# Turned probabilities in two single banks, and a scheduler with other costs, in an encoder-decoder layer

## The chip, the cores and the metric

The kernel runs on one core of a Trainium2 chip. The metric is the device time of one execution in microseconds (us). The time of the kernel before is the median of three runs.

## The reference

The reference is one encoder layer over a short context (2 x 77 x 512) and one decoder layer over a long input `x` (2 x 2048 x 512), all in float32, with 16 heads of 32 and a feed-forward width of 2048. What it computes, cut to its core:

```python
eb = _rel_bias(enc_rel, Ts, Ts)
x = src                                    # the context, 77 rows
x = x + _mha(ln1(x), ln1(x), enc_in, enc_out, eb)
x = x + relu(ln2(x) @ enc_ff1.T + b) @ enc_ff2.T + b
memory = x
sb = _rel_bias(dec_rel_self, Tt, Tt) + causal
cb = _rel_bias(dec_rel_cross, Tt, Ts)
y = tgt                                    # the input, 2048 rows
y = y + _mha(ln1(y), ln1(y), dec_sa_in, dec_sa_out, sb)
y = y + _mha(ln2(y), memory, dec_ca_in, dec_ca_out, cb)
y = y + relu(ln3(y) @ dec_ff1.T + b) @ dec_ff2.T + b
return y

# _mha: q, k, v projections; scores = q @ k.T / sqrt(32) + bias;
# softmax over the keys; times v; output projection
```

The relative bias has one value for all keys at a distance of 128 rows or more, so only the last two key tiles of a query tile need a bias of their own.

## The kernel before, in words

**Stages.** The causal self-attention comes first, with the encoder, the projections and the layer norms placed among its work. The cross attention and the feed-forward follow; there the products are done in seven instead of eight block products, with TensorE as one full array. In the profile the first stage ends at about 1560 us.

**Units.** The self-attention is cut into 128 units: two batches, four blocks of 512 rows (`m`), four groups of four heads (`g`) and four tiles of 128 query rows (`t`). A unit of block `m` and tile `t` has 4m + t + 1 key tiles, so the largest have 16, which is 2048 keys; the last unit, number 127, is one of these. Each unit goes through four kinds of work:

- *score* (`scores`, line 1002): for up to four key tiles, one matmul for each of the four heads, each on 32 rows of the array and into a bank of PSUM of its own, so four banks at a time. DVE then moves each bank into the area `pp` and keeps the running maximum (its tiles `pp` and `mx`); after the last piece it forms the negative maximum `nm`.
- *exp*: one ACTIVATE for each head on ACT, over all keys of the unit, in place in `pp`.
- *turn* (`turn`, line 1057): for up to two key tiles, the probabilities of four heads are transposed on TensorE, 64 query rows at a time, 16 transposes in all. The lower and the upper 64 rows go to two banks. Each bank is copied into its half of a tile `pts`, by ACT or by DVE (`copy` offers both).
- *value* (`values`, line 1081): for the same key tiles, matmuls with 32 output rows for each head, all of a group into one bank that stays held over the group's four units.

TensorE so works in four tilings: 64x128 for transposes, 32x128 for scores, 128x32 for values and projections, and 128x128. In the profile a matmul in float32 counts as two instructions, a transpose as one.

**Banks.** PSUM has eight banks of 512 columns. `Places` (its `grab` is line 128) hands them out when a task starts. A slot of two places takes an even-odd pair where one is free and comes free as a whole; a slot of one takes a place whose neighbour is taken, where there is one. A place comes free when the last task that uses the slot has ended.

**Who sets the order.** Nothing in the kernel's text fixes the order of the work. A `Tape` records every operation as part of a task, with the tasks that it depends on. A task has a kind, a unit and a part of the unit, and these give its key through the table `PLAN`. Then `plan` (line 402) runs the tasks through a clock of its own, on the host, before anything is built: SyncE, ACT, DVE and GpSimd take the ready task of the lowest key in `pick` (line 514); TensorE has one candidate for each tiling in `choices` (line 532), and for each of them, and for two short pauses, `ahead` (line 562) plays the next 20 us and adds up the work that TensorE, DVE and ACT would get done. The best is taken. The result is one fixed order of instructions for each engine, which `run` emits; all of them therefore carry line 360 in the profile. The chip never consults the planner: its costs act only through the order, and through the choice between ACT and DVE for some evictions.

What the planner believes of the chip stands in a few constants: `cost_of` (line 227) for durations; `SWITCH` (line 60), added to a task of TensorE whose tiling differs from that of the one before; `LATER` (line 61), the time from a task's end until another engine can use its result; and in `start` (line 585) one queue for transfers, each with 1300 ns to begin, its bytes at 190 a nanosecond, and 700 ns to land. `PLAN` holds nine sets of parameters, one for each 16 units and one for what follows.

Of the kernel before, what the change touches and what calls it, by code (L numbers as in the profile page):

```python
# [43 lines left out]
for _n, _w in _VECS:  # L44
# [15 lines left out]
SWITCH = {(32, 128): 217, (128, 32): 139, (64, 128): 140, (128, 128): 217}  # L60
LATER = {"PE": 212, "DVE": 130, "ACT": 150, "POOL": 110, "SP": 60}
# [4 lines left out]
LOOK = {"look":20000.0,"pause":(150.0,400.0)}  # L66
PLAN = [
    {"window": 6.9, "hold": 2.5, "flex": 271,
     "stay": {(64, 128): 0.463, (128, 32): 0.15, (32, 128): 0.337, (128, 128): 0.322},
     "keys": {"score": (-2.08, 0.76), "exp": (-0.5, 0.2), "turn": (0, 0.93), "value": (1.75, 1.12), "light": (-0.98, 0.02), "job": (0.33, 0.33), "late": (-0.6, 0), "stats": (-0.5, 0), "load": (0.04, 0.13), "ff": (0.42, 0), "side": (-0.28, 0)}},  # L70
    {"window": 5.9, "hold": 1.59, "flex": 305,
     "stay": {(64, 128): 0.588, (128, 32): 0.35, (32, 128): 0.195, (128, 128): 0.33},
     "keys": {"score": (-2.65, 0.76), "exp": (-0.19, 0.2), "turn": (0, 1.0), "value": (0.7, 1.56), "light": (-0.37, 0.02), "job": (0.45, 0.31), "late": (-0.6, 0), "stats": (-0.5, 0), "load": (0.04, 0.38), "ff": (-0.32, 0), "side": (-0.47, 0)}},
    {"window": 3.5, "hold": 0.97, "flex": 234,
     "stay": {(64, 128): 0.588, (128, 32): 0.462, (32, 128): 0.782, (128, 128): 0.322},
     "keys": {"score": (-2.44, 0.76), "exp": (0.02, 0.2), "turn": (0, 0.86), "value": (0.7, 0.96), "light": (-0.1, 0.02), "job": (0.16, 0.31), "late": (-0.6, 0), "stats": (-0.5, 0), "load": (0.03, 0.38), "ff": (-0.32, 0), "side": (-0.28, 0)}},
    {"window": 6.6, "hold": 0.89, "flex": 54,
     "stay": {(64, 128): 0.362, (128, 32): 0.368, (32, 128): 0.375, (128, 128): 0.259},
     "keys": {"score": (-2.91, 0.87), "exp": (-0.28, 0), "turn": (0, 0.86), "value": (1.16, 1.46), "light": (-0.37, 0.02), "job": (0.29, 0.31), "late": (-0.6, 0), "stats": (-0.5, 0), "load": (0.06, 0.38), "ff": (-0.32, 0), "side": (-0.28, 0)}},
    {"window": 6.5, "hold": 2.17, "flex": 34,  # L80
     "stay": {(64, 128): 0.36, (128, 32): 0.35, (32, 128): 0.195, (128, 128): 0.33},
     "keys": {"score": (-2.08, 0.76), "exp": (-0.19, 0.2), "turn": (0, 0.86), "value": (0.83, 1.56), "light": (-0.37, 0.02), "job": (0.45, 0.31), "late": (-0.6, 0), "stats": (-0.5, 0), "load": (0.04, 0.38), "ff": (-0.32, 0), "side": (-0.87, 0)}},
    {"window": 5.9, "hold": 2.46, "flex": 117,
     "stay": {(64, 128): 0.36, (128, 32): 0.35, (32, 128): 0.195, (128, 128): 0.633},
     "keys": {"score": (-2.65, 0.76), "exp": (-0.19, 0.2), "turn": (0, 0.89), "value": (0.7, 1.56), "light": (-0.37, 0.02), "job": (0.45, 0.31), "late": (-0.6, 0), "stats": (-0.5, 0), "load": (0.04, 0.38), "ff": (0.17, 0), "side": (-0.47, 0)}},
    {"window": 5.2, "hold": 0.97, "flex": 259,
     "stay": {(64, 128): 0.396, (128, 32): 0.462, (32, 128): 0.782, (128, 128): 0.322},
     "keys": {"score": (-2.44, 0.76), "exp": (0.02, 0.2), "turn": (0, 0.86), "value": (0.7, 0.96), "light": (-0.1, 0.02), "job": (0.16, 0.31), "late": (-0.6, 0), "stats": (-0.5, 0), "load": (0.03, 0.38), "ff": (-0.32, 0), "side": (-0.28, 0)}},
    {"window": 3.5, "hold": 0.89, "flex": 54,
     "stay": {(64, 128): 0.362, (128, 32): 0.368, (32, 128): 0.375, (128, 128): 0.259},  # L90
     "keys": {"score": (-2.91, 0.87), "exp": (-0.28, 0), "turn": (0, 0.86), "value": (1.16, 1.46), "light": (-0.37, 0.02), "job": (0.29, 0.31), "late": (-0.6, 0), "stats": (-0.5, 0), "load": (0.06, 0.38), "ff": (-0.32, 0), "side": (-0.28, 0)}},
    {"window": 5.9, "hold": 1.95, "flex": 305,
     "stay": {(64, 128): 0.214, (128, 32): 0.35, (32, 128): 0.195, (128, 128): 0.33},
     "keys": {"score": (-2.65, 0.76), "exp": (-0.19, 0.2), "turn": (0, 0.97), "value": (0.7, 1.56), "light": (-0.37, 0.02), "job": (0.45, 0.31), "late": (-0.6, 0), "stats": (-0.5, 0), "load": (0.04, 0.38), "ff": (-0.32, 0), "side": (-0.47, 0)}},
]
# [27 lines left out]
class Places:  # L123
# [103 lines left out]
def cost_of(engine, op, a, k):  # L227
    out = a[0]
    F = max(free_of(x) for x in a[:2] if is_ap(x))
    if engine == "PE":  # L230
# [5 lines left out]
        stream, load = n * 2 / 2.4, 63 if passes == 1 else 117 * cols / P  # L236
# [54 lines left out]
class Tape:  # L291
# [70 lines left out]
    def prepare(self):  # L362
# [10 lines left out]
        for t in tasks:  # L373
# [11 lines left out]
            t.by = dict(t.ways)  # L385
# [6 lines left out]
            if t.ways[0][0] == "SP":  # L392
                a = t.ways[0][1][0][2][0]
                t.size = free_of(a) * a.shape[0] * 4
# [7 lines left out]
    def plan(self, parts, look=0.0, weights=(1.0, 0.5, 0.5), pause=()):  # L402
# [3 lines left out]
        for t in tasks:  # L406
            t.todo, t.came, t.at = len(t.before), 0.0, None
            kind, n, part = t.kind
            t.part = parts[min(max(int(n), 0) // (NC * TB), len(parts) - 1)]
            first, wide = t.part["keys"][kind]  # L410
            t.key = n + first + wide * part
# [5 lines left out]
        self.left = sorted(tasks, key=lambda t: (t.key, t.order))  # L417
        run = Run(self)
        for t in tasks:
            if not t.todo:  # L420
                run.ready(t)
        gain = dict(zip(("PE", "DVE", "ACT"), weights))
        while len(run.order) < len(tasks):
            run.step_events()
            while True:
# [6 lines left out]
                if look:  # L432
                    best = None
                    for t in found + list(pause if len(found) > 1 or found[0].mode != run.mode else ()):
                        mark = run.save()
                        score = run.ahead(t, look, gain)
# [3 lines left out]
                    run.take(best[1])  # L440
# [6 lines left out]
class Run:  # L447
# [3 lines left out]
    def __init__(self, tape):  # L451
        self.tape, self.left, self.floor, self.now = tape, tape.left, 0, 0.0
# [3 lines left out]
        self.mode, self.dma, self.share, self.period, self.worked = None, 0.0, 0.5, 0, {}  # L456
        self.events, self.frees, self.order, self.log = [0.0], [], [], None
        self.places = list({id(s.places): s.places for s in tape.slots}.values())

    def save(self):  # L460
        self.log = []
        return (
            self.floor, self.now, dict(self.free), dict(self.port), {e: list(v) for e, v in self.lists.items()}, self.mode, self.dma,
# [4 lines left out]
    def back(self, mark):  # L468
# [3 lines left out]
        (self.floor, self.now, self.free, self.port, self.lists, self.mode, self.dma, self.share, self.period, self.worked,  # L472
# [41 lines left out]
    def pick(self, e):  # L514
# [3 lines left out]
        limit, now = low.key + low.part["window"], self.now  # L518
        shut = e in self.port and self.port["DVE" if e == "POOL" else "POOL"] > now
        for key, _, t in self.lists[e]:  # L520
            if key > limit:
                return None
            if t.came > now or shut and e in t.port or any(u.seen > now and u.by != e for u in t.banks):
# [3 lines left out]
            if e == "DVE" and len(t.ways) > 1 and self.free["ACT"] < now + low.part["flex"]:  # L527
# [4 lines left out]
    def choices(self):  # L532
# [3 lines left out]
        rule, now = low.part, self.now  # L536
        limit, stay, hold = low.key + rule["window"], rule["stay"], rule["hold"]
        wait, found = {}, {}
        for key, _, t in self.lists["PE"]:
            if key > limit:  # L540
                break
            if t.came > now or any(u.seen > now and u.by != "PE" for u in t.banks):
# [12 lines left out]
    def take(self, first):  # L555
        if isinstance(first, float):
# [28 lines left out]
    def start(self, e, t):  # L585
# [3 lines left out]
        took = t.spans[e]  # L589
        if e == "PE":  # L590
# [5 lines left out]
            at, stop, p = now, now + took, int(now // PERIOD)  # L596
            while at < stop:
                to = max(at, min(stop, (p + 1) * PERIOD))
                self.worked[p] = self.worked.get(p, 0.0) + (to - at) * t.dense
                at, p = to, p + 1  # L600
            if t.mode != self.mode:
                self.mode = t.mode
                took += SWITCH[t.mode]
        end = t.until = now + took
# [6 lines left out]
        seen = end + LATER[e]  # L611
        if e == "SP":
            self.dma = max(self.dma, now + 1300) + t.size / 190.0
            seen = self.dma + 700
        for u in t.banks:
            put(u, "by", e)
            put(u, "seen", seen)
        for s in t.fresh:
            put(s, "at", s.places.grab(s.n))
        for s in t.slots:  # L620
            put(s, "left", s.left - 1)
            if not s.left:
                heapq.heappush(self.frees, (seen, id(s), s))
        events = self.events
        heapq.heappush(events, seen)
        heapq.heappush(events, end)
        for w in t.after:
            came = end if e in w.own else seen
# [7 lines left out]


# [43 lines left out]
def tile_encoder_decoder(ctx: ExitStack, tc: tile.TileContext, ins, out):  # L681
# [102 lines left out]
    with (  # L784
# [272 lines left out]
        def turn(n, k0, kn):  # L1057

            pts = turned_places.take(kn)
            rows = P // 2  # L1060
            pair = bank(2)
# [1225 lines left out]
```

## Time and profile before

| what | value |
|---|---|
| median of three runs | 2637.32 us (2636.71 to 2638.04) |
| the profiled execution's own time | 2637.01 us |
| its span, first to last instruction | 2635.2 us |
| mean granted clock of TensorE | 0.997 |
| TensorE busy | 2607.7 us, 99% of the span |
| DVE, ACT, GpSimd busy | 1789.6, 1506.8, 774.5 us |

The profile is of one execution. Its page gives each engine's busy time, the chain of work that ended last, and groups of instructions with their mean duration and the idle time before them. Matmuls are pipelined and their ends are modelled: the end of a run of matmuls lies some way after the start of the next run, so that a change of tiling shows as busy time, and only a longer wait as idle time. The pitch of matmuls is therefore read from start to start. A row of the timeline merges instructions of one group that follow each other.

### The profile page before, as it was taken

What the parts mean: (1) busy time and instruction counts of PE and PEld (TensorE: products, weight loads), DVE (VectorE), ACT (ScalarE), POOL (GpSimd) and SP (SyncE); (2) the same over time, 40 slices, a digit from 0 to 9 for tenths busy, and PEclk for the clock granted to TensorE, in tenths of its full rate; (3) what the DMA queues carried; (4) which work ended last, traced back from release to release, by engine and by line L of the source; (5) the groups of instructions that cost most, each with busy time, mean ns of one, the idle gap of its engine ahead of it and who ended that gap; (6) DMA issues with size and microseconds to landing.
All of it is one profiled execution on the core that took longest, in us unless ns stands there. A gap on an engine that the chain in (4) does not pass through costs nothing.

```text
span 2635.2 us, 83740 instructions
## 1 busy us (share of the span) xinstructions
PE 2607.7 (99%) x35326; PEld 1777.3 (67%) x35326; DVE 1789.6 (68%) x5181; ACT 1506.8 (57%) x2890; POOL 774.5 (29%) x697
## 2 busy tenths in 40 slices
PE   9999999999999999999999999999999999999999
PEld 4456555555555455555555667888888888888898
DVE  4776588888887687788788874647373737373634
ACT  2665478778877567678778764343434343434331
POOL 1110151100001011202000013828374746465546
PEclk9999999999999999999999999999999999999999
DMA  8333363310115222423010244545556554545466
GB/s 220 94 92 110 113 187 99 103 54 19 42 46 138 81 70 62 152 80 118 23 46 18 77 141 133 179 154 167 166 160 186 162 175 151 180 145 172 141 204 200
DMA packets 252714, 320.28 MB, mean 122 GB/s; under 512 B 29569, under 2 KB 142513, under 8 KB 252211
## 3 DMA queue, kind: packets, MB, share of 16 engines
q1 hardware_dynamic: 252338, 314.93, 39.2%
q8 instruction: 278, 4.55, 0.7%
q14 instruction: 98, 0.79, 0.1%
HBM read 274.91 MB, written 39.95 MB: 119 GB/s over the span
## 4 chain that ended last, share of the span: by engine, by line
PE 93%; DVE 4%; ACT 2%; issue 1%; POOL 0%; DMA 0%; POOLq 0%; DVEq 0%; ACTq 0%
PE psum L360 93%; DVE pp L360 3%; ACT pp L360 1%; DVE pts L360 1%; ACT nT L360 0%; POOL pp L360 0%; ACT pts L360 0%; DVE oT L360 0%; DMA xt<-in_x_dram 0%; DVE bnst L360 0%; POOL vv L360 0%; ACT kT L360 0%; DVE nm L360 0%; DVE xr L360 0%; DVE kT L360 0%
## 5 line engine op out<-in xcount | busy, mean ns | idle before, releaser
L360 ACT ACTIVATE pp<-pp,nm 128x128 f32<-128x128 f32 (+15 forms) x512 | 615.0, 1209 | 115.6 <-DVE nm L360 114.2
L360 DVE TENSOR_SCALAR_CACHE_REDUCE pp<-psum 128x512 f32<-128x512 f32 (+3 forms) x1024 | 561.6, 591 | 129.6 <-PE psum L360 128.1
L360 ACT COPY pts<-psum 128x512 f32<-128x512 f32 (+2 forms) x785 | 405.4, 571 | 277.1 <-PE psum L360 229.4
L360 PEld LDWEIGHTS psum<-ident,pp 64*128 64x128 f32 (+1 forms) x8904 | 320.6, 139 | 189.6 <-issue 67.0
L360 PE MATMUL psum<-ident,pp 64*128 64x64 f32 (+1 forms) x8904 | 381.2, 228 | 8.8 <-DVE pp L360 4.1
L360 POOL TENSOR_TENSOR pp<-pp 128x512 f32<-128x512 f32 (+1 forms) x196 | 264.3, 1358 | 359.4 <-DMA pp<-in_dec_ff_wT_dram 169.7
L360 DVE COPY pts<-psum 128x512 f32<-128x512 f32 (+2 forms) x479 | 298.8, 657 | 80.5 <-PE psum L360 75.5
L360 PE MATMUL psum<-pp 128*128 128x128 f32 (+4 forms) x2984 | 352.5, 282 | 0.2 <-DVE oT L360 0.2
L360 PEld LDWEIGHTS psum<-pp 128*128 128x128 f32 (+3 forms) x2984 | 334.0, 190 | 23.7 <-issue 13.9
L360 PE MATMUL psum<-kT,q 32*128 32x512 f32 (+3 forms) x2560 | 334.3, 575 | 3.1 <-DVE pp L360 1.7
L360 PE MATMUL psum<-pts,vv 128*32 128x128 f32 x8704 | 319.6, 277 | 3.8 <-ACT pts L360 1.7
L360 PEld LDWEIGHTS psum<-pts,vv 128*32 128x32 f32 x8704 | 220.0, 109 | 113.7 <-issue 80.6
L360 PE MATMUL psum<-vv,pp 128*128 128x256 f32 (+1 forms) x1072 | 256.4, 390 | 0.0
L360 PE MATMUL psum<-nT,wqk 128*32 128x512 f32 x2048 | 244.2, 603 | 2.7 <-ACT pp L360 1.5
L360 PEld LDWEIGHTS psum<-vv,pp 128*128 128x128 f32 (+1 forms) x1072 | 198.0, 188 | 40.5 <-issue 15.2
L360 DVE CUSTOM_DVE_ANT_0 pp<-psum,bias 128x256 f32<-128x256 f32 (+1 forms) x512 | 196.1, 411 | 13.0 <-PE psum L360 12.9
L360 DVE TENSOR_TENSOR oT<-psum,oT 128x256 f32<-128x256 f32 (+2 forms) x260 | 106.2, 424 | 135.4 <-PE psum L360 86.3
L360 PEld LDWEIGHTS psum<-kT,q 32*128 32x128 f32 x2560 | 109.0, 183 | 107.5 <-issue 41.0
L360 DVE TENSOR_TENSOR kT<-kT,psum 128x512 f32<-128x512 f32 x96 | 64.6, 679 | 164.6 <-PE psum L360 163.2
L360 PE MATMUL psum<-nT,pp 128*128 128x256 f32 x768 | 174.8, 381 | 0.0
L360 PEld LDWEIGHTS psum<-nT,pp 128*128 128x128 f32 x768 | 144.2, 190 | 21.2 <-issue 1.9
L360 POOL TENSOR_TENSOR rstd<-rstd,mhalf 128x1 f32<-128x1 f32 x32 | 18.3, 571 | 467.7 <-DVE rstd L360 455.3
(136 smaller groups left out, 3119.0 us busy)
## 6 DMA issues: line engine op xcount, KB each, us to landing
pp<-w_d SPq DMA_DIRECT2D x520, 256.0 KB, 2.8
pp<-in_dec_ff_wT_dram SPq DMA_DIRECT2D x112, 256.0 KB, 3.7
wqk<-in_dec_sa_in_wT_dram SPq DMA_DIRECT2D x64, 256.0 KB, 2.9
bias<-tzg SPq DMA_DIRECT2D x128, 128.0 KB, 3.4
wbig<-in_dec_sa_in_wT_dram SPq DMA_DIRECT2D x8, 1024.0 KB, 5.3
vv<-in_enc_ff_wT_dram SPq DMA_DIRECT2D x8, 1024.0 KB
wbig<-in_dec_sa_out_wT_dram SPq DMA_DIRECT2D x8, 1024.0 KB, 6.2
vv<-y SPq DMA_DIRECT2D x32, 256.0 KB, 3.9
```

What stands on the lines that cost most here:

```text
L360: getattr(getattr(self.nc, engine), op)(*map(real, a), **{n: real(v) for n, v in k.items()})
```

## The change

Two things change.

The first is in the attention. A turn takes two slots of one bank each instead of one slot of two. The transposes, the copies and their data are the same; each bank has its own slot, so each comes free with its own copy, and the two need not be neighbours.

The second is in the planner alone. `SWITCH` and `LATER` are gone. In their place:

- a matmul task starts no sooner than its inputs, its banks and the places it takes allow, plus the time to load its first weights (`t.load`); after another tiling also no sooner than the last task's end plus `TAIL` of that tiling plus `DRAIN`;
- the end of a task becomes known after `DONE` of its engine (plus `TAIL` on TensorE), and each engine hears of it after its own `HEARD`;
- a transfer takes its bytes at 300 a nanosecond plus a share for short runs of contiguous bytes, after 1200 ns instead of 1300;
- the costs of transposes and of short matmuls differ a little;
- `PLAN` has 56 entries, one for each four units. Their numbers are those of the nine sets before, repeated. The keys of all tasks are now computed from the entry of the phase that the planner is in, and again when the next phase is entered; before, each task kept the key of its own set. Where only one candidate stands, nothing is played ahead.

```diff
-SWITCH = {(32, 128): 217, (128, 32): 139, (64, 128): 140, (128, 128): 217}
-LATER = {"PE": 212, "DVE": 130, "ACT": 150, "POOL": 110, "SP": 60}
+DRAIN = 93
+TAIL = {(32, 128): 21, (128, 32): 21, (64, 128): -3, (128, 128): 0}
+DONE = {"PE": 165, "DVE": 82, "ACT": 108, "POOL": 48, "SP": 0}
+HEARD = {"PE": 30, "DVE": 45, "ACT": 45, "POOL": 60, "SP": 60}
...
-        return got
+        return max(free[i] for i in got), got
...
-        stream, load = n * 2 / 2.4, 63 if passes == 1 else 117 * cols / P
+        stream, load = n * 2 / 2.4, cols / 2.4 + 10 if passes == 1 else 117 * cols / P if n > 77 else 104
...
+            if t.mode:
+                _, op, a, _ = t.ways[0][1][0]
+                t.load = free_of(a[1]) / 2.4 + 10 if op == "transpose" else free_of(a[1]) * 2 / 2.4
...
+                    t.size += size / 300 + 0.3 * size / run
...
+            low = run.rule()
+            if low is not None and low.phase > phase:
+                phase = low.phase
+                run.enter(phases[phase])
...
+            for u in t.banks:
+                if u.by != "PE":
+                    since = max(since, u.seen + HEARD["PE"])
             if t.mode != self.mode:
+                since = max(since, self.over + TAIL.get(self.mode, 0) + DRAIN)
                 self.mode = t.mode
-                took += SWITCH[t.mode]
-        end = t.until = now + took
+            at = max(now, since + load)
+            self.over = end = at + took
+            lag += TAIL[t.mode]
...
-        seen = end + LATER[e]
+        done = end + lag
         if e == "SP":
-            self.dma = max(self.dma, now + 1300) + t.size / 190.0
-            seen = self.dma + 700
+            self.dma = max(self.dma, now + 1200) + t.size
+            done = self.dma + 700
...
-            came = end if e in w.own else seen
+            came = end if e in w.own else done + w.hears
...
-            pair = bank(2)
+            two = [bank(), bank()]
...
-                        nc.tensor.transpose(pair[:, a, ts(x, rows)], src[at], ident[at, at])
+                        nc.tensor.transpose(two[a][:, ts(x, HALF)], src[at], ident[at, at])
...
-        order = nc.plan(PLAN, **LOOK)
+        order = nc.plan(PLAN, STEP)
```

More of the change, by code (lines that the diff above doesn't have):

```diff
@@ L98, with phase_of @@
+STEP = 4
+MODES = ((64, 128), (128, 32), (32, 128), (128, 128))
+KINDS = ("score", "exp", "turn", "value", "light", "job", "late", "stats", "load", "ff", "side")
+def phase_of(window, hold, flex, stay, first, wide, look, pause, weights):
+    return {
+        "window": window, "hold": hold, "flex": flex, "stay": dict(zip(MODES, stay)),
+        "keys": dict(zip(KINDS, zip(first, wide))), "look": look, "pause": pause, "weights": weights,
+    }
+PLAN = [phase_of(*x) for x in (
[112 rows of a table added]
+)]
 class View:
@@ L421, in plan @@
                 run.ready(t)
-        gain = dict(zip(("PE", "DVE", "ACT"), weights))
         while len(run.order) < len(tasks):
             run.step_events()
+            low = run.rule()
+            if low is not None and low.phase > phase:
+                phase = low.phase
+                run.enter(phases[phase])
+            part = run.part
             while True:
@@ L431, in plan @@
                     break
-                if look:
+                if part["look"]:
                     best = None
-                    for t in found + list(pause if len(found) > 1 or found[0].mode != run.mode else ()):
+                    tries = found + list(part["pause"] if len(found) > 1 or found[0].mode != run.mode else ())
+                    for t in tries if len(tries) > 1 else ():
                         mark = run.save()
-                        score = run.ahead(t, look, gain)
+                        score = run.ahead(t, part["look"], {"PE": 1.0, "DVE": part["weights"][0], "ACT": part["weights"][1]})
                         run.back(mark)
@@ L522, in pick @@
                 return None
-            if t.came > now or shut and e in t.port or any(u.seen > now and u.by != e for u in t.banks):
+            if t.came > now or shut and e in t.port or any(u.seen + HEARD[e] > now and u.by != e for u in t.banks):
                 continue
@@ L526, in pick @@
                 continue
-            if e == "DVE" and len(t.ways) > 1 and self.free["ACT"] < now + low.part["flex"]:
+            if e == "DVE" and len(t.ways) > 1 and self.free["ACT"] < now + self.part["flex"]:
                 continue
@@ L535, in choices @@
             return []
-        rule, now = low.part, self.now
+        rule, now = self.part, self.now
         limit, stay, hold = low.key + rule["window"], rule["stay"], rule["hold"]
@@ L541, in choices @@
                 break
-            if t.came > now or any(u.seen > now and u.by != "PE" for u in t.banks):
+            if t.came > now or any(u.seen + HEARD["PE"] > now and u.by != "PE" for u in t.banks):
                 continue
@@ L588, in start @@
         t.calls, t.engine = t.by[e], e
-        took = t.spans[e]
+        took, lag = t.spans[e], DONE[e]
+        since = t.came
+        for s in t.fresh:
+            at, got = s.places.grab(s.n)
+            since = max(since, at)
+            put(s, "at", got)
         if e == "PE":
@@ L622, in start @@
             if not s.left:
[L623 to L626, printed above, removed]
+                freed = True
+                heapq.heappush(self.frees, (done + HEARD["PE"], id(s), s))
+        if freed or t.banks:
+            heapq.heappush(events, done + HEARD["PE"])
+            heapq.heappush(events, done + HEARD["DVE"])
         for w in t.after:
-            came = end if e in w.own else seen
+            came = end if e in w.own else done + w.hears
             if came > w.came:
```

102 lines of the change are left out of this document (42 added, 60 removed), and 112 rows, old and new, of the table PLAN.

## The prediction

> **What bounds the kernel now.** I read the page first: TensorE is busy for 99% of the span, and it is 93% of the chain that ended last.
>
> ```profile
> span 2635.2 us, 83740 instructions
> PE 2607.7 (99%) x35326; PEld 1777.3 (67%) x35326; DVE 1789.6 (68%) x5181; ACT 1506.8 (57%) x2890; POOL 774.5 (29%) x697
> ...
> PE 93%; DVE 4%; ACT 2%; issue 1%; POOL 0%; DMA 0%; POOLq 0%; DVEq 0%; ACTq 0%
> ...
> L360 ACT COPY pts<-psum 128x512 f32<-128x512 f32 (+2 forms) x785 | 405.4, 571 | 277.1 <-PE psum L360 229.4
> ...
> L360 DVE COPY pts<-psum 128x512 f32<-128x512 f32 (+2 forms) x479 | 298.8, 657 | 80.5 <-PE psum L360 75.5
> ...
> pp<-w_d SPq DMA_DIRECT2D x520, 256.0 KB, 2.8
> ```
>
> Second, the busy time by stretches (columns: PE, weight loads, DVE, ACT, POOL, granted clock, DMA share, GB/s). Up to 1560 us runs the attention that the change touches; after it the feed-forward.
>
> ```profile
> 14.00:130.00 116.00, 110.52 (x1456) 52.81 (x1452) 69.60 (x267) 58.51 (x175) 16.07 (x16) 0.94 0.57 149
> 130.00:400.00 270.00, 268.93 (x4845) 153.75 (x4839) 185.42 (x658) 161.24 (x331) 54.96 (x54) 1.00 0.42 127
> 400.00:800.00 400.00, 396.58 (x7165) 224.86 (x7161) 334.46 (x1088) 311.65 (x492) 29.78 (x34) 1.00 0.19 57
> 800.00:1200.00 400.00, 398.24 (x6482) 206.74 (x6480) 310.62 (x1085) 281.65 (x597) 67.14 (x75) 1.00 0.33 99
> 1200.00:1440.00 240.00, 238.47 (x4284) 133.63 (x4284) 201.08 (x668) 183.79 (x287) 11.19 (x12) 1.00 0.16 51
> 1440.00:1560.00 120.00, 116.10 (x2284) 72.95 (x2276) 103.53 (x328) 96.61 (x141) 5.11 (x4) 1.00 0.23 76
> 1560.00:2500.00 940.00, 940.00 (x7834) 804.98 (x7835) 517.43 (x969) 376.87 (x795) 514.46 (x438) 1.00 0.53 164
> 2500.00:2635.20 135.20, 128.76 (x936) 118.25 (x934) 59.63 (x100) 31.48 (x69) 71.26 (x53) 0.99 0.63 201
> ```
>
> Length less PE gives PE's idle time: 5.5, 1.1, 3.4, 1.8, 1.5 and 3.9 us in the attention, 17.2 in all; none from 1560 to 2500; 6.4 after it, the last results' way out, which nothing here touches. Third, who ended TensorE's waits from 13.6 to 1560 us (total, times, longest):
>
> ```profile
> PE psum L360 <- DVE pp L360: 4.4, 12, 0.9
> PE psum L360 <- ACT pts L360: 3.4, 8, 0.7
> PE psum L360 <- ACT pp L360: 2.2, 4, 1.5
> PE psum L360 <- DVE mx L360: 1.4, 4, 0.5
> ...
> PE psum L360 <- DVE pts L360: 0.8, 2, 0.6
> ```
>
> So there are two things to win: these few waits, and the gaps between tilings, which the page counts as busy. The timeline at the end of the attention prices the gaps (start, length, engine, work, matmuls):
>
> ```profile
> 1539.95 0.71 PE L360 MATMUL psum<-ident,pp 64*128 64x64 f32 x16
> ...
> 1540.59 0.65 PE L360 MATMUL psum<-pts,vv 128*32 128x128 f32 x16
> ...
> 1541.17 1.14 PE L360 MATMUL psum<-kT,q 32*128 32x512 f32 x8
> ...
> 1542.24 1.08 PE L360 MATMUL psum<-pts,vv 128*32 128x128 f32 x32
> ...
> 1543.78 2.35 PE L360 MATMUL psum<-kT,q 32*128 32x512 f32 x8 [0.47 <-DVE pp L360]
> ...
> 1546.06 1.26 PE L360 MATMUL psum<-ident,pp 64*128 64x64 f32 x32
> ...
> 1548.04 0.64 PE L360 MATMUL psum<-pts,vv 128*32 128x128 f32 x16 [0.71 <-ACT pts L360]
> ...
> 1548.82 2.04 ACT L360 ACTIVATE pp<-pp,nm 128x2048 f32<-128x2048 f32 x1
> ...
> 1550.82 1.09 ACT L360 COPY pts<-psum 128x512 f32<-128x512 f32 x2
> 1551.34 1.09 PEld L360 LDWEIGHTS psum<-ident,pp 64*128 64x128 f32 x32 [0.20 <-issue]
> 1551.34 1.22 PE L360 MATMUL psum<-ident,pp 64*128 64x64 f32 x32
> ...
> 1552.49 1.08 PE L360 MATMUL psum<-pts,vv 128*32 128x128 f32 x32
> ...
> 1553.51 0.46 PE L360 MATMUL psum<-ident,pp 64*128 64x64 f32 x8
> ...
> 1555.54 1.90 PE L360 MATMUL psum<-wbig,oT 128*32 128x512 f32 x16
> ...
> 1555.75 2.03 ACT L360 ACTIVATE pp<-pp,nm 128x2048 f32<-128x2048 f32 x1
> ...
> 1557.37 0.40 PE L360 MATMUL psum<-ident,pp 64*128 64x64 f32 x6
> ...
> 1557.92 2.06 PE L360 MATMUL psum<-ident,pp 64*128 64x64 f32 x58 [0.15 <-ACT pp L360]
> ```
>
> From start to next start, 16 transposes take 0.64 us and 32 take 1.15, so 0.032 each and 0.13 fixed for a run. Values: 0.58 for 16 and 1.02 for 32, so 0.14 fixed. A projection: 16 in 1.83, with 0.14 off 0.42 for four at a time; eight score matmuls then stream in 0.84 and took 1.07: 0.23 fixed. The full array:
>
> ```profile
> 1753.94 1.89 PE L360 MATMUL psum<-nT,pp 128*128 128x256 f32 x8
> 1755.76 1.13 PE L360 MATMUL psum<-pts,bias 32*128 32x77 f32 x32
> 1756.82 5.45 PE L360 MATMUL psum<-nT,pp 128*128 128x256 f32 x24
> 1762.11 3.19 PE L360 MATMUL psum<-vv,pp 128*128 128x256 f32 x14
> ```
>
> Its 24 take 5.29 and its 8 take 1.82, so 0.217 each, and 0.08 is over at a run's head and 0.08 at its end: 0.16.
>
> **The change part by part.** No arithmetic is added or removed: both orders hold the same matmuls, copies and transfers. What moves is the order, and which of DVE and ACT does some copies.
>
> *Changes of tiling.* I count them in the two orders: 1419 before, 1390 after. Runs of 64-row transposes go from 451 to 441, of 128x32 from 527 to 497, of 32x128 from 346 to 349, of 128x128 from 95 to 103. So -10 x 0.13 - 30 x 0.14 + 3 x 0.23 + 8 x 0.16 = -3.5 us. All lies on TensorE, which is the path, so it counts in full unless a wait takes its place (rivals). Bounds: 29 fewer at 0.13 is -3.8; with the eight runs of the full array at 0.23 it is -3.0.
>
> *Single banks.* A turn (16 transposes) now gives back each bank after its own copy, 0.57 or 0.66 us, instead of both after the later one. No instruction is added. The waits that it could shorten are those that end on copies or on score evictions, 3.4 + 0.8 + 4.4 + 1.4 = 10.0 us. Against it, the planner takes the freed bank at once: between a turn's last use of a bank and the next use lie 29.3 matmuls in the order before and 30.0 in that after, on average, so a bank gets no less time to be emptied. What grows is the room elsewhere: from a turn to the product that reads it 59.6 matmuls before and 63.3 after, with 16 or fewer in 19 cases before and 11 after; from a unit's last score to its first turn a median of 120 before and 136 after. I take 8/19 off the waits for turned copies (-1.8) and 16/136 off the 8.0 us that end on DVE's pp and mx and on ACT's pp (-0.9): -2.7 us. Bounds: all 10.0 gone; or, since both engines' queues are redrawn, the 36 waits half as many again, +8.
>
> *New constants of the planner* (drain and tail by pair, first load, DONE and HEARD, transfers). They cost nothing on the chip; their effect is the order already counted. The transfers' queue is redrawn too. No wait of TensorE in the stretch above ends on a DMA, and a block of weights lands 2.8 us after its issue; that price per late block is the end above, zero the end I take, since the DMA share in the attention is 0.16 to 0.57.
>
> *Moved copies.* 14 evictions of 512 columns go from DVE to ACT, and two turned copies on balance the other way. At 0.6 us that is 7 us of each engine's 1500, beside 16% idle DVE and 22% idle ACT in 400 to 800: nothing.
>
> *The last unit.* Unit 127 has no successor to hide its softmax. Before, its last scores end at 1546.06 and its first turn is free at 1557.92, after four exps of which the first starts at 1548.82 and the last ends at 1557.78, with two copies (1.09) among them. In the order after, no copy stands between these exps, so 10.8 us. But only 16 values, 32 transposes, 32 values, 24 transposes, 56 values and 16 of a projection lie between: 0.58 + 1.15 + 1.02 + 0.90 + 1.68 + 1.83 = 7.2 us. So 3.6 us are bare. Before, the same way gives 10.0 us of work in 11.8, 1.8 bare. The 64 transposes that moved ahead of the last scores cover there 0.47 and the about 1.2 by which those scores ran over 1.07 (2.35 from row to end). Net from +0.1 to +2.9 (copies still in the way: +1.1 more); I take the middle, +1.5.
>
> *The start.* Between 14 and 130 us the granted clock is 0.94, so 7 us went to slow stretches. Their place depends on the mix of small tiles, which is redrawn; I take no change, with 3.5 us either way.
>
> Sum: -3.5 - 2.7 + 1.5 = -4.7 us on a profiled execution of 2637.0 us (span 2635.2 and 1.8 around it): 2632.3, say 2632. The median of the three runs is 2637.3, 0.3 above that execution, so 0.2% less.
>
> **A rule weighed.** The longest wait in the list is 1.5 us (on ACT's pp), and from 14 to 130 the clock fell all the same. The Trainium skill, "TensorE: Matmul & The Clock Gate" (HAM oscillation), asks only that idle gaps stay below some 3.4 us. By it the start would lose nothing, before or after, and the sum stays; by the trace thin work is enough, hence the 3.5 us both ways.
>
> **The rivals.** *The copies bind, and what is saved becomes waiting.* From 1440 to 1560 DVE is busy 103.5 of 120 us and ACT 96.6. If evictions set the pace, fewer changes of tiling only bring TensorE sooner to a wait: the -3.5 and -2.7 go, the +1.5 stays, 2638.5. Against it: 400 to 800 is as full on DVE (84%) and TensorE idles there 3.4 of 400. The Trainium skill states this rule in "TensorEngine Tiling (Array Packing)", PSUM Bottleneck: tiling speeds up the matmuls and not the emptying of PSUM. The trace bears it out in the last 120 us alone.
>
> *Slower: scores starve.* A score takes four banks at once; turns that pick up single banks as they come free can keep four from being free together, and scores slip until DVE and ACT run dry. A wait on DVE's pp costs 4.4/12 = 0.37 us. From 29 more of them, among 320 score pieces, the kernel is 0.2% slower (2642.6); with one in six pieces (53) hit, 2632 + 19.6 = 2652. For it: pairs were kept whole before. Against it: the room from score to turn grew.
>
> *A larger gain.* Half of the 15.7 us of listed waits goes (they are 36, few and large, which better due times would avoid): 2637.0 - 3.5 - 7.9 + 1.5 = 2627.
>
> **How the numbers follow.** 0.2% (5.3 us) is about what a measurement of this kernel can tell from no change. The forecast, 2632 and its own 2628 to 2636, 0.43; it lies astride the bound, half each side. The copies bind, 2636 to 2642: 0.21. A larger gain, below 2628: 0.18. Slower by starving scores or by a start that fares worse, above 2642.6: 0.18. Faster 0.21 + 0.18 and a little of the forecast's better half, 0.42; same 0.40; slower 0.18. The range leaves out the far half of the last two: 2622 to 2647.
>
> **What would show it.** TensorE's idle time from 14 to 1560 us at 12 to 17 us instead of 17.2; waits on ACT's and DVE's pts below 4.2 us; one bare stretch of 3 to 4 us before the last unit's first turn; feed-forward unchanged with no idle time from 1560 to 2500. Waits on DVE's pp above 10 us would mean starving scores; a clock below 0.94 in the first 130 us, a worse start; waits that end on a DMA, that the transfers' new cost misleads the planner. Each would make the prediction wrong.

## The result, and the profile after

The changed kernel takes 2643.61 us, the median of nine runs (2641.92 to 2644.76); the kernel before, on the same chips, takes 2635.36 (nine runs, 2633.11 to 2638.04). The ratio is 1.003, with a 95% interval from 1.0019 to 1.004: slower by 8.2 us, or 0.3%. The forecast was faster by 0.2%. The profiled execution of the changed kernel took 2642.32 us, its span 2640.5, against 2635.2 before; so the two traces hold 5.3 of the 8.2 us.

The page of the changed kernel shows that TensorE's busy time fell, 2602.0 us after 2607.7. In these two traces the loss is all idle time: 38.5 us after 27.5.

```profile
span 2640.5 us, 83665 instructions
...
PE 2602.0 (99%) x35326; PEld 1780.5 (67%) x35326; DVE 1762.2 (67%) x5167; ACT 1513.5 (57%) x2904; POOL 780.0 (30%) x697
```

The busy time by stretches, with the columns of the table before:

```profile
14.00:130.00 116.00, 108.95 (x1524) 53.22 (x1520) 68.96 (x274) 61.38 (x182) 16.03 (x16) 0.97 0.55 149
130.00:400.00 270.00, 266.28 (x4830) 153.57 (x4820) 184.08 (x637) 164.47 (x341) 54.06 (x52) 1.00 0.45 132
400.00:800.00 400.00, 391.71 (x7046) 222.82 (x7044) 330.54 (x1085) 307.49 (x479) 30.49 (x36) 1.00 0.18 53
800.00:1200.00 400.00, 398.80 (x6540) 208.19 (x6544) 313.79 (x1098) 280.04 (x593) 66.57 (x74) 1.00 0.34 98
1200.00:1440.00 240.00, 237.77 (x4256) 135.85 (x4256) 198.99 (x656) 184.32 (x287) 11.72 (x12) 1.00 0.17 53
1440.00:1560.00 120.00, 116.02 (x2254) 72.55 (x2246) 102.31 (x333) 96.54 (x139) 5.13 (x4) 1.00 0.25 78
1560.00:2500.00 940.00, 938.98 (x7818) 802.33 (x7819) 492.48 (x954) 379.86 (x801) 516.37 (x434) 1.00 0.53 163
```

Length less PE: 7.1, 3.7, 8.3, 1.2, 2.2 and 4.0 us, 26.5 in the attention where it was 17.2. The largest growth stands in 400 to 800, from 3.4 to 8.3. The list of what ended TensorE's waits in the attention of the changed kernel (total, times, longest) names it:

```profile
PE psum L457 <- ACT nT L457: 6.2, 10, 1.0
PE psum L457 <- DVE oT L457: 3.7, 5, 1.0
PE psum L457 <- DVE pp L457: 3.1, 6, 1.7
PE psum L457 <- ACT pp L457: 2.9, 2, 1.7
PE psum L457 <- DVE nT L457: 2.5, 3, 1.2
...
PE psum L457 <- DVE pts L457: 1.3, 2, 1.1
...
PE psum L457 <- ACT pts L457: 1.1, 5, 0.3
PE psum L457 <- DMA wqk<-in_dec_sa_in_wT_dram: 1.0, 1, 1.0
```

The waits that the change was to touch are short: 2.4 us on turned copies instead of 4.2, 3.1 on score evictions instead of 4.4. New are the waits on the tiles `nT` and `oT`: 6.2 + 3.7 + 2.5 = 12.4 us in 18. In the same list of the kernel before they are these two rows, 1.9 us in 4, which the prediction passed over:

```profile
PE psum L360 <- ACT nT L360: 1.4, 3, 0.6
...
PE psum L360 <- DVE nT L360: 0.5, 1, 0.5
```

`nT` is a normed and transposed tile, `oT` a unit's transposed output. Both are evicted from slots of two banks that the change does not touch. So instructions that the diff leaves as they were now end the largest share of the waits.

### The profile page after: what moved, and what is told of

It reads as the page before. It is cut to its first block, busy times and chain, and to the rows that moved or that the text cites. A ratio compares the mean times of both kernels' runs of the same rounds, so it can differ in the third digit from the quotient of the medians.

```text
span 2640.5 us, 83665 instructions
## 1 busy us (share of the span) xinstructions
PE 2602.0 (99%) x35326; PEld 1780.5 (67%) x35326; DVE 1762.2 (67%) x5167; ACT 1513.5 (57%) x2904; POOL 780.0 (30%) x697
## 4 chain that ended last, share of the span: by engine, by line
PE 93%; DVE 3%; ACT 1%; DMA 1%; issue 1%; SPq 0%; POOLq 0%; POOL 0%; DVEq 0%; ACTq 0%
PE psum L457 93%; DVE pp L457 2%; ACT pp L457 1%; DVE pts L457 0%; DMA wqk<-in_dec_sa_in_wT_dram 0%; DMA pp<-in_ctx_dram 0%; ACT pts L457 0%; ACT nT L457 0%; DVE oT L457 0%; DMA kT<-in_rel_dram 0%; SPq L457 0%; DVE cmx L457 0%; DVE nT L457 0%; DVE nm L457 0%; ACT oT L457 0%
## 5 line engine op out<-in xcount | busy, mean ns | idle before, releaser
L457 PE MATMUL psum<-kT,q 32*128 32x512 f32 (+3 forms) x2560 | 340.6, 578 | 6.1 <-DVE oT L457 2.2
L457 POOL TENSOR_TENSOR xr<-xr,row_dec_sa_out_b 128x512 f32<-128x512 f32 x30 | 38.4, 1282 | 461.9 <-DMA xr<-in_x_dram 461.9
```

The lines of the kernel that those rows point to most:

```text
L457: getattr(getattr(self.nc, engine), op)(*map(real, a), **{n: real(v) for n, v in k.items()})
```

## The experiments

**What an `nT` wait is.** This is one of them in the timeline of the changed kernel (start, length, engine, work, and in brackets the idle time before it):

```profile
454.03 0.46 PE L457 MATMUL psum<-ident,xt 64*128 64x64 f32 x8
...
454.42 1.93 PE L457 MATMUL psum<-wbig,oT 128*32 128x512 f32 x16
...
456.48 1.05 DVE L457 TENSOR_SCALAR nT<-psum,vecs 128x128 f32<-128x128 f32 x3 [1.05 <-PE psum L457]
...
457.59 1.92 PE L457 MATMUL psum<-wbig,oT 128*32 128x512 f32 x16 [1.24 <-DVE nT L457]
...
459.58 0.41 DVE L457 TENSOR_SCALAR nT<-psum,vecs 128x128 f32<-128x128 f32 x1 [2.05 <-PE psum L457]
460.14 1.14 PE L457 MATMUL psum<-kT,q 32*128 32x512 f32 x8 [0.63 <-DVE nT L457]
```

Eight transposes of `xt` end at 454.49; their four evictions into `nT` need nothing else. Yet DVE waits 1.05 us until the 16 matmuls of a projection have ended, does three, and waits 2.05 us for the next 16; and these 16 wait for the three. By the kernel's data flow the two have nothing to do with each other: the projection reads `oT` and writes a bank of its own. The order as planned tells what they share. The slot of the transposes was dealt the banks 0 and 4, and both halves of the projection write bank 2. Each eviction reads its two banks in one access with a stride, and the program treats it as if it held the banks between as well. The program built from the changed kernel has these waits in it: the first eviction waits for the last matmul of the projection's first half, the second half waits for the third eviction, and the fourth eviction waits for the last matmul of the second half. In the program with these pairs as neighbours (the next run), where the slot has the banks 2 and 3 and the projection bank 4, the first eviction waits for the last transpose alone, and the second half for no eviction. The planner counts only the two banks.

A slot of two places takes an even-odd pair where one is free, and any two otherwise. Of the 136 slots of two that are no turns, 17 lie on banks that aren't neighbours before the change, and 24 after (12 and 18 of the 76 of the norms and outputs in the attention). These are called far pairs below (spanned slots in the expectations). With either part of the change alone there are 22. To test the theory I dealt the bank numbers of all slots again after planning, with the order of every engine, the engines and the times of each slot kept. Nothing else differs. The rival is that the waits come from the new order alone.

```diff
         order = nc.plan(PLAN, STEP)
+        recolor(order, banks, True)     # True: neighbours; False: far apart
         nc.run(order)
...
+def recolor(order, places, near):
+    ...   # slots in the order of use; a bank may be taken when free by the plan's clock
+                if wide:              # a slot of two that is no turn
+                    c += (at[1] - at[0] - 1) if near else (7 - at[1] + at[0])
```

*The changed kernel, pairs as neighbours* (2 of 136 are not).

> The order of instructions on every engine is that of the changed kernel; only the numbers of the PSUM banks are dealt out anew, so that a slot of two banks holds neighbours: 2 of 136 such slots span a foreign bank instead of 24. Theory (spanned banks): an eviction that reads two banks in one access is held back by, and holds back, matmuls in the banks that lie between; without them the waits of TensorE on the evictions into nT and oT fall from 12.4 us to under 4 and the time from 2643.6 to 2634 to 2638 us. Rival (the new costs made a worse plan): waits and time stay, 2642 to 2645 us.

Measured: 2629.87 us (11 runs), a ratio of 0.9977 (0.9968 to 0.9986) to the kernel before; 13.7 us less than the changed kernel, and 4 us below the range that was expected. In the two traces the span is 11.5 us less, and 8.0 of these are busy time:

```profile
span 2629.0 us, 83679 instructions
...
PE 2594.0 (99%) x35326; PEld 1772.8 (67%) x35326; DVE 1761.2 (67%) x5167; ACT 1512.2 (58%) x2904; POOL 780.3 (30%) x697
```

In its timeline the same place is one run of matmuls and one of evictions:

```profile
451.18 0.46 PE L492 MATMUL psum<-ident,xt 64*128 64x64 f32 x8
...
451.57 3.64 PE L492 MATMUL psum<-wbig,oT 128*32 128x512 f32 x32
...
452.50 1.36 DVE L492 TENSOR_SCALAR nT<-psum,vecs 128x128 f32<-128x128 f32 x4
```

In its waits `nT` and `oT` have 2.0 us in 3 left, of 12.4 in 18. The waits on turned copies, though, are 9.5 us in 29 where they were 2.4 in 7, with no instruction moved:

```profile
PE psum L492 <- ACT pts L492: 6.4, 23, 0.7
PE psum L492 <- DVE pts L492: 3.1, 6, 1.4
...
PE psum L492 <- DVE oT L492: 1.1, 1, 1.1
...
PE psum L492 <- ACT nT L492: 0.9, 2, 0.6
```

*The kernel before, every such pair as far apart as the order allows* (all 136).

> The order of instructions on every engine is that of the kernel before; the slots of two banks are dealt out as far apart as can be: all 136 span foreign banks instead of 17, 76 of them in the attention instead of 12. Theory (spanned banks): 64 more spanned slots at about 0.75 us of TensorE's waits each (6.0 us in 8 waits in the changed kernel) make 30 to 60 us, so 2665 to 2700 us. Rival (the numbers of the banks do not matter): 2634 to 2638 us.

Measured: 2778.49 us, a ratio of 1.0539 (1.0524 to 1.0553). Bank numbers alone cost 143 us, more than either theory said. Its page and its waits in the attention's first 1565 us:

```profile
span 2771.9 us, 83774 instructions
...
PE 2645.7 (95%) x35326; PEld 1787.5 (64%) x35326; DVE 1797.1 (65%) x5181; ACT 1516.1 (55%) x2890; POOL 773.5 (28%) x697
```

```profile
PE psum L395 <- ACT nT L395: 49.1, 49, 3.0
PE psum L395 <- DVE oT L395: 24.0, 26, 3.2
PE psum L395 <- ACT pp L395: 15.7, 14, 3.1
PE psum L395 <- DVE nT L395: 10.4, 8, 2.0
```

The waits on `nT` and `oT` are the same ones, grown to 83.5 us; DVE's and ACT's busy time is within 0.7% of the kernel before (1797.1 and 1516.1), and an eviction into `nT` keeps its length (the rows stand in the last section). What is bought with a far pair is a wait.

*The kernel before, pairs as neighbours* (1 of 136 is not).

> The order of the kernel before, with the banks dealt out anew so that 1 slot of two banks spans foreign banks instead of 17. Theory (spanned banks): the waits on nT and oT were 1.9 us in 4, so a gain of 1 to 4 us, 2632 to 2635 us beside 2635.8. Rival (spanned banks do harm only in the changed order): 2635 to 2637 us.

Measured: 2631.65 us, a ratio of 0.9983 (0.9974 to 0.9992), at the edge of the theory's range. So far pairs cost the kernel before 3.9 us, and the changed kernel 13.7: of the loss of 8.2 they explain 9.9, more than all. The rest of the change must then have been a small gain; the next runs take it apart. The page of this run is needed below:

```profile
span 2628.7 us, 83793 instructions
...
PE 2601.9 (99%) x35326; PEld 1773.9 (67%) x35326; DVE 1790.5 (68%) x5181; ACT 1506.3 (57%) x2890; POOL 774.4 (29%) x697
```

**The two parts of the change.** The planner alone, with turns in pairs as before, and the single banks alone, with the planner of before; each as it is dealt and with neighbours.

```diff
-            two = [bank(), bank()]          # planner alone: the changed kernel with the turn of before
+            pair = bank(2)
...                                          # and its transposes and copies
-            pair = bank(2)                  # single banks alone: the kernel before with the changed turn
+            two = [bank(), bank()]
...
```

> The new planner with turns in one slot of two banks, as before. 16 spanned slots in the attention (12 before, 18 after), 1402 changes of tiling. Theory (spanned banks): most of the loss is there without single banks, 2639 to 2643 us. Rival (single banks cause it): 2632 to 2637 us. Rival (the new costs cause it): 2643 us or more.

Measured: 2648.32 us, a ratio of 1.0044 (1.0032 to 1.0057), above the range of the theory and in that of the new costs: the new planner is no gain by itself.

> The planner of before with its constants, and turns in two single banks. 17 spanned slots in the attention, 1412 changes of tiling. Theory (spanned banks): 2638 to 2643 us. Rival (the new costs cause it): 2632 to 2637 us. Rival (single banks cause it by themselves): 2643 us or more.

Measured: 2635.88 us, a ratio of 1.0 (0.9991 to 1.0009), as the kernel before, with 22 far pairs for its 17. This too is where the rival of the new costs had it. But both runs hold far pairs, and the next two take these out: what the single banks gain is spent there.

> The new planner with turns in pairs (2648.3 us as it was), its order kept, banks dealt out anew: 1 spanned slot instead of 22. Theory (spanned banks explain the loss): the 5.8 us of waits on nT and oT go, 2640 to 2643 us, which leaves 10 us between this and the changed kernel with neighbours (2629.9): the worth of single banks under this planner. Rival (spanned banks explain all): 2630 to 2635 us.

Measured: 2637.95 us, a ratio of 1.0008 (0.9999 to 1.0017), between the two ranges. Far pairs cost the new planner 10.4 us even with turns in pairs.

> The old planner with turns in single banks (2635.9 us as it was), its order kept, banks dealt out anew: 1 spanned slot instead of 22. Theory (spanned banks): the 8.1 us of waits on nT and oT go, 2627 to 2630 us, no worse than the changed kernel with neighbours (2629.9), so that the gain is the single banks' and the new costs add nothing. Rival (the new costs add a gain of their own): 2633 us or more.

Measured: 2621.47 us (2620.88 to 2624.86), a ratio of 0.9951 (0.9938 to 0.9963). It is the fastest kernel of the study, and 5.5 us below the range that was expected; far pairs cost this order 14.4 us. With neighbours the single banks gain 10.2 us under the old planner (2631.65 to 2621.47) and 8.1 under the new one (2637.95 to 2629.87); the new planner loses 6.3 with pairs (2631.65 to 2637.95) and 8.4 with single banks (2621.47 to 2629.87). The prediction had the new order gain by its changes of tiling, and the last expectation had the new costs add nothing. So this was open: what in the planner loses?

**What in the planner loses.** My first reading was from the waits. With the old planner (single banks, neighbours) the waits for turned copies are these, 2.0 us in 8; with the new one they are the 9.5 us in 29 shown above:

```profile
PE psum L395 <- ACT pts L395: 1.5, 7, 0.3
...
PE psum L395 <- DVE pts L395: 0.5, 1, 0.5
```

So the costs seemed to believe that copies are heard too early. The rival was the other edit, the keys of all tasks computed again at each phase. Two runs separate them, and two more, called jogs here, tell how far the time moves when one constant of the planner moves by 2 ns. All four have single banks and neighbours.

```diff
 def enter(self, part):
...
-            first, wide = part["keys"][kind]
+            first, wide = PLAN[t.phase]["keys"][kind]   # new costs, each task its own keys
```

> The changed kernel with its banks re-dealt, and one more undo: each task keeps the key of its own entry of the table for good, as before the change, instead of having it computed again at each phase. The new costs stay. 1396 changes of tiling, 1 slot of two banks that are not neighbours. Compared with 2629.9 (both new) and 2621.5 (both old), banks re-dealt in each. Theory, the costs mislead (copies are believed to be heard early, so products are placed too close): the loss stays, 2627 to 2633. Rival, the keys of the phase do it: 2620 to 2625. Third, any redrawn order loses against one whose parameters were fitted to it: somewhere from 2624 to 2634, with no telling which.

Measured: 2622.93 us (2620.97 to 2624.66), a ratio of 0.995 (0.9937 to 0.9962). This is in the range of the rival, and below that of the third theory. The loss is gone, though the waits for turned copies are still there, 8.2 us in 29:

```profile
PE psum L492 <- ACT pts L492: 6.2, 24, 0.7
...
PE psum L492 <- DVE pts L492: 2.0, 5, 0.7
```

So that reading of the waits falls. Nor do the new costs place products closer to their copies: by the orders, a mean of 61.3 matmuls lies here between a turn and its product, and 59.8 with the old costs. The waits for copies come with less busy time, 2590.1 us here against 2598.8 with the old costs. By the prediction's prices, 1396 changes of tiling instead of 1412 make some 2 of these 9 us (an estimate); the rest is open.

```profile
span 2619.0 us, 83681 instructions
...
PE 2590.1 (99%) x35326; PEld 1771.9 (68%) x35326; DVE 1761.8 (67%) x5165; ACT 1511.7 (58%) x2906; POOL 779.4 (30%) x697
```

So the new costs come out even. The other half puts the new keys into the old planner, and with them the other parameters of the phase's set, which in the run above stayed with the phase:

```diff
-            t.key = n + first + wide * part          # once, from the task's own set
...
+            low = run.rule()
+            if low is not None and low.phase > phase:
+                phase = low.phase
+                run.enter(parts[phase])              # all keys, from the phase's set
```

> The other half: the costs of before, turns in single banks, banks re-dealt, and the keys of all tasks computed again from the set of the phase that the planner is in. 1421 changes of tiling, 2 slots of two banks that are not neighbours. If the costs mislead: 2619 to 2625, as without the new keys (2621.5). If the keys do it: 2627 to 2633. If any redrawn order loses: 2624 to 2634.

Measured: 2627.36 us (2626.05 to 2628.56), a ratio of 0.9966 (0.9952 to 0.9979); 1421 changes of tiling instead of 1412. The keys lose 5.9 us here, and 6.9 with the new costs. This fits the keys and a redrawn order alike; the jogs are to part them.

The two jogs:

```diff
-LATER = {"PE": 212, "DVE": 130, "ACT": 150, ...
+LATER = {"PE": 212, "DVE": 130, "ACT": 152, ...    # old costs and keys
...
-DONE = {"PE": 165, "DVE": 82, "ACT": 108, ...
+DONE = {"PE": 165, "DVE": 82, "ACT": 110, ...      # new costs and keys
```

> How much the time moves when the order is redrawn for no reason: the best version so far (costs and keys of before, single banks, banks re-dealt, 2621.5), with one constant of the planner moved by 2 ns (LATER of ACT from 150 to 152). 1410 changes of tiling, 1 slot that is not of neighbours. If a cause in the new costs or keys makes the 8 us: 2619 to 2624. If any redrawn order loses: 2625 to 2632.

Measured: 2623.18 us (2622.38 to 2625.97), 1.7 above its unjogged twin; the ranges overlap.

> The same on the other side: the changed kernel with its banks re-dealt (2629.9), with DONE of ACT moved from 108 to 110. 1390 changes of tiling, 2 slots that are not of neighbours. If a cause in the new costs or keys makes the 8 us: 2627 to 2633. If orders scatter by several us whatever the costs: as likely 2622 to 2627 as above.

Measured: 2630.13 us (2627.8 to 2632.9), 0.3 above its twin. So these two redrawn orders moved the time by less than 2 us. They are small redraws, though: on TensorE 3 and 4% of the tasks stand at another place than in the twin, against 15 and 16% for the keys and 54% for the new costs, which came out even. That the 6 to 7 us of the keys are no scatter rests on both pairs losing about the same, and how far a redraw of that size scatters was not tried.

Where the keys lose can be followed by units. The end of the last product of a unit in the run with new costs and new keys lies behind that of its own-keys twin by 1.0 us at unit 32, 2.6 at unit 40, 6.2 at unit 48, 6.3 at unit 64, 7.5 at unit 112 and 10.0 at unit 127. (These two traces lie 10.0 us apart, the medians 6.9.) Units 32 and 48 are where sets change. There all waiting tasks get the keys of the new set, those of the units behind and those of the units ahead; before, the two sets stood side by side. But the other pairs don't bear this place out: with the old costs the same reading gives 0.7, 0.7, -0.3, 2.6, 2.2 and 4.8 us, and the jog of the new costs lies 2.8 to 3.1 us behind its twin at units 32 to 48 and 0.8 at unit 127. Why the keys make a worse order, I did not find. With the new costs the idle time in the attention is 6.3 us larger in many small waits, and no single one carries it; with the old costs it is the same (13.2 us after 13.0). So the keys' loss is measured, and its mechanism is open.

**The account.** With each pair as neighbours: single banks -10.2, new costs +1.5 (2621.47 to 2622.93, as little as the jog's 1.7), new keys +6.9 (2622.93 to 2629.87). Far pairs as in the kernels: +13.7 after, +3.9 before, so +9.9 by unrounded medians. Sum: -10.2 + 1.5 + 6.9 + 9.9 = +8.1 us; the measured difference is 8.2. The terms are steps from one run to the next, so their sum has to close and proves nothing; what carries them is that single banks, keys and far pairs were each measured in more than one place, with the same sign.

## Why the prediction was wrong

*What failed.* The new order was priced by its changes of tiling and by mean distances between tasks, and two of its costs were in no term. The first belongs to the step "Single banks". It priced the time that a bank has to be emptied, and a rival the four banks that scores need, but not which numbers are left for the other slots of two. This is not a term of wrong size, it was missing: nobody in the list of rivals waited for `nT`. The rows were in the trace, 1.4 and 0.5 us, and the code said that a slot of two takes any two places where no pair is free. The runs showed +9.9 us in its place, 13.7 after against 3.9 before, which is more than the whole loss. It is not the single banks' alone: the new planner with turns in pairs pays 10.4 us for far pairs as well. The second belongs to the step "New constants of the planner": "their effect is the order already counted". The constants themselves came out near nothing, +1.5 us. The keys, which stand in the change and have no term, cost 6.9 us with the new costs and 5.9 with the old. The count doesn't carry that: with the keys there are 1390 changes of tiling instead of 1396 with the new costs, and 1421 instead of 1412 with the old. A count of an order does not carry its waits.

*Changes of tiling*, -3.5. No pair of runs bears it out by itself. Busy time fell by 5.7 us in the profile, but bank numbers alone, with the same order and so the same count, moved it as much: from 2607.7 to 2601.9 in the kernel before and from 2602.0 to 2594.0 in the changed one. And with neighbours the planner alone, which makes 1402 changes instead of 1419, is as busy as the kernel before (2602.5 and 2601.9).

*Single banks*, -2.7. The sign was right and the size was too small: -10.2 and -8.1 in the two pairs of runs with neighbours. Of the 10.2, the two profiled executions show 5.6 (spans 2628.7 and 2623.1): 3.1 less busy time and the rest less idle. In the changed kernel the waits on turned copies fell to 2.4 us, which is what the step's -1.8 would leave of 4.2, but that is luck. With neighbours on both sides they are 4.5 us before (3.4 + 1.1) and 9.5 after, so the wider room between turn and product saved none of them; in the changed kernel the waits for `nT` and `oT` seem to have come in their place. The waits on score evictions and exps went from 8.0 to 7.3.

*The last unit*, +1.5. By the prediction's own window, from the run behind the unit's last scores to its first free turn, it took 11.86 us before (1546.06 to 1557.92) and 11.29 after (1548.88 to 1560.17). TensorE was idle for 0.97 us of it before and for 3.24 after, most of that in these rows:

```profile
1554.78 1.90 PE L457 MATMUL psum<-wbig,oT 128*32 128x512 f32 x16
1556.61 0.34 PE L457 MATMUL psum<-ident,pp 64*128 64x64 f32 x4
1558.18 0.28 PE L457 MATMUL psum<-ident,pp 64*128 64x64 f32 x2 [1.23 <-ACT pp L457]
1560.17 2.46 PE L457 MATMUL psum<-ident,pp 64*128 64x64 f32 x58 [1.71 <-ACT pp L457]
```

That is +2.3, inside the bounds of +0.1 and +2.9 and nearer to the upper one: two waits of 1.23 and 1.71 us where one bare stretch of 3 to 4 was forecast. The mechanism was right. The four exps ran without a copy between them, as the step said.

*Moved copies* and *the start*. Most of the moved evictions go into `kT` and `oT`, and no row of TensorE's waits ends on ACT's work into these. DVE's busy time fell by 27 us, more than 14 evictions make up. 25 of these lie from 1560 to 2500 us, where TensorE idles 1.0 us in 940; why they went is open. At the start the idle time rose from 5.5 to 7.1 while the clock rose from 0.94 to 0.97, within the 3.5 us given.

*The rivals.* Scores did not starve: waits on DVE's `pp` fell to 3.1 us, where above 10 was the mark. The copies did not bind: waits on `pts` were below the 4.2 that was the mark, and where they are above it, at 9.5 with neighbours, the kernel is 13.7 us faster. The kernel is slower by another way than the one named. The mark that did speak was the idle time of 14 to 1560 us, 26.5 us where 12 to 17 were forecast. The transfers' one wait, 1.0 us for `wqk`, is small.

## What to carry to other kernels

Before breaking a resource into smaller pieces, look at who still takes it in larger ones, and what numbers are left for them; an access over two banks that aren't neighbours tied itself here to the banks between. The changed kernel won 13.7 us by other bank numbers alone. Compare two planned orders by running them: fewer changes of tiling came with more time here (1390 with 2629.87 us, 1412 with 2621.47), and a wait list that looked like the cause (turned copies) was still there when the cause was gone. And when a change has two parts with opposite signs, run each with the suspected side effect taken out, since 10 us of gain were hidden under 14 of loss.

## What was not expected of the hardware and the program

Bank numbers alone, with the same instructions in the same order on every engine, moved the time from 2631.65 to 2778.49 us. The evictions themselves kept their length: those into `nT` took 455 ns each on ACT with far pairs and 466 with neighbours, from 14 to 1500 us (the first row is of far pairs):

```profile
L395 ACT ACTIVATE nT<-psum,vecs 128x128 f32<-128x128 f32 x99 | 42.3, 455 | 73.6 <-PE psum L395 60.7 <-DVE pp L395 6.1 <-DVE mx L395 2.7
L395 ACT ACTIVATE nT<-psum,vecs 128x128 f32<-128x128 f32 x97 | 36.9, 466 | 10.0 <-PE psum L395 9.9
```

So the price lies in the waits that are written into the program, and in what follows from them. Of the 143 us between the two traces, 99 are idle time of TensorE and 44 busy time. The Trainium skill, "PSUM — Partial Sum Buffer" (PSUM bank collisions raise a hardware error), asks to keep two engines apart by bank, and says that accesses to different banks run clean; by it, bank 2 need not wait for a read of banks 0 and 4. No run here shows that: a kernel without these waits was not tried. With the far pairs the mean granted clock was 0.984, after 0.998 with neighbours; TensorE's busy time rose by 44 us (2601.9 to 2645.7) with the same matmuls. The Trainium skill, "TensorE: Matmul & The Clock Gate" (HAM oscillation), ties the lower clock to idle gaps above some 3.4 us. The longest wait in this run's rows is 3.2 us, and the clock fell all the same; what lowered it, no run here tells.
